# Sums of the MLP's weights: made once by GpSimd during attention and kept in DRAM, instead of made by GpSimd in every pass of the MLP

## The chip, the cores and the metric

The kernel runs on one core of a Trainium2 chip. The metric is the device time of one execution in microseconds. Everything is in float32. In the text PE is TensorE, DVE VectorE, ACT ScalarE, POOL GpSimd, and SP the queue from which nearly all DMAs are issued. L833 means line 833 of the kernel before.

## The reference, cut to what matters

An image of 48 x 48 tokens with 768 channels goes through a transformer block and then through a Fourier layer. The block is the part that the change touches:

```python
xn = layernorm(x, ln1_g, ln1_b)
q, k, v = split(xn @ qkv_w + qkv_b)                  # 12 heads of 64
attn = softmax(q * scale @ k.T + rel_h + rel_w)      # 2304 x 2304 per head
x = x + (attn @ v) @ proj_w + proj_b
xn2 = layernorm(x, ln2_g, ln2_b)
h = gelu(xn2 @ mlp_w1 + mlp_b1)                      # 2304 x 3072
x = x + (h @ mlp_w2 + mlp_b2)                        # 2304 x 768
# then: rfft2, two blockwise complex layers with relu and softshrink, irfft2, + x
```

## The kernel before

The program has five stages, one after the other, with the profile's times in microseconds: queries, keys and values (0 to 404), attention (404 to 1411), the projection (1411 to 1580), the MLP with the forward row transform (1580 to 2590), and the Fourier layer (to 2833).

**Seven products instead of eight.** The large matrix products cut both operands into 2 x 2 blocks and form the result from seven block products, not eight (the Strassen-Winograd scheme). For that, each operand needs sums and differences of its blocks. `left` (L160) makes those of a left operand with four additions, `right` (L166) those of a right operand: three new blocks, and one block that is overwritten. A weight chunk that is ready for use is thus seven blocks: four of the matrix (one of them overwritten) and three sums.

**Attention** is a loop over 6 pairs of heads (`pr`) and, within a pair, 6 groups of 384 queries (`c`), 36 iterations. An iteration has 18 steps `kt`. In each, PE makes the scores of 128 keys in `sp` (L670 content, L679 position, the latter from the tile `terms`), and ACT writes their exponentials to `exps`, which lies in `main` (L689). After every second step DVE adds two steps' exponentials into `pairs` (L833), and at the end the two halves of `pairs` into `acc` (L837). Then PE multiplies the exponentials with the values (L702) in six portions of three steps. Between the portions stands other work, by a table that `between` (L785) makes: before portion 1 DVE transposes `acc` and reduces it to `part` (`denominators`, L720 and L722); before portion 4 PE adds up the denominators with a small matmul that reads `part` (L731), DVE takes their reciprocal `rden` (L733), and POOL adds it to `inverse` (L735), which a later test for overflow reads; before portion 5 SP writes `rden` to DRAM (`den_d`, L749), stores an earlier result to `oT` (L783), and loads a broadcast of the reciprocals (`spread`, L762), after which DVE scales (L774) and POOL adds a bias (L777). The last of these stores is issued from POOL. For c below 3, and for c of 4 and 5 for the next pair, `relative` prepares the position terms of a coming iteration: matmuls into the one small PSUM bank, copies by ACT, a subtraction by DVE (L242), and 24 DMAs from SP for each `terms` (L309, L313), three buffers. The queries, keys and values of the next pair are loaded at c = 1 and c = 3.

**The order of work.** PE and SP keep the order of the program text throughout attention, and ACT and DVE in the loop, as the text asks for it (`manual_schedule`). POOL is not in that list during attention; a scheduler places its instructions. In the projection and in the MLP POOL is in the list.

**The projection** adds `proj_b` to the input on POOL (`residual`, L857) and then adds the products to that.

**The MLP** makes 3 passes of 768 tokens (`p`), each over 12 chunks of 256 hidden units (`n`). `weights(p, n)` (L1260) loads a chunk of `mlp_w1` (L1263) and one of `mlp_w2` (L1270), 768 KB each, and has POOL make the sums with `left` and `right`, eight additions of 128 x 384. Each chunk is loaded and summed anew in every pass. `hidden(p, n)` (L1280) makes seven products of three matmuls each (L1291), applies gelu (L1297) with the bias of two 128-unit tiles, `2 * n` and `2 * n + 1`, and has DVE make the sums of its result (`hs`). `added(p, n, i)` (L1333) multiplies with the chunk of `mlp_w2` (L1351, L1355) for three groups of tokens, and DVE adds to `x1` (L1353). It runs one chunk behind `hidden`, interleaved with it. The weight tiles have two buffers each, so that a chunk's loads are issued about a chunk ahead.

Of the kernel before, what the change touches and what calls it, by code (L numbers as in the profile page):

```python
# [19 lines left out]
P = 128  # L20
# [3 lines left out]
C = 768  # L24
# [3 lines left out]
FF = 4 * C  # L28
FCH = 256
TB = 768  # L30
G = 384
# [15 lines left out]
def block_then_afno(  # L47
# [6 lines left out]
    proj_w,  # L54
    mlp_w1,
    mlp_w2,
    vecs,
# [47 lines left out]
    stat_d = [dram.tile([12, P], F32, name=f"stat_d{p}") for p in range(T // TB)]  # L105
    den_d = dram.tile([NC * (T // G), 2 * G], F32, name="den_d")

    big1 = ctx.enter_context(tc.tile_pool(name="big1", bufs=1))
# [51 lines left out]
    def left(eng, a11, a12, a21, a22, s):  # L160
        eng.tensor_tensor(s[0], a21, a22, ALU.add)
        eng.tensor_tensor(s[1], s[0], a11, ALU.subtract)  # L162
        eng.tensor_tensor(s[2], a12, s[1], ALU.subtract)
        eng.tensor_tensor(a21, a11, a21, ALU.subtract)

    def right(eng, b11, b12, b21, b22, t):  # L166
# [28 lines left out]
    with ExitStack() as flag_scope:  # L195
# [12 lines left out]
        with ExitStack() as att:  # L208
# [444 lines left out]
            with tc.manual_schedule(engines={mybir.EngineType.PE, mybir.EngineType.SP}):  # L653
# [126 lines left out]
                def stored(queue=nc.sync):  # L780
                    while results:
                        pr, c, o = results.pop(0)
                        queue.dma_start(out=oT[ts(pr, P), ts(c, G)], in_=o)  # L783

                def between(pr, c, acc):  # L785

                    last = pr == NC - 1
                    work = {
                        1: [partial(denominators, pr, c, acc)],
                        4: [partial(inverses, pr, c)],  # L790
# [24 lines left out]
                with tc.manual_schedule(  # L815
                    engines={mybir.EngineType.Activation, mybir.EngineType.DVE}
                ):
                    for pr in range(NC):
                        for c in range(T // G):
# [8 lines left out]
                            pairs = o_pool.tile([P, 2, 2, G], F32, name="pairs", bufs=1)  # L828
                            for kt in range(NT):
                                scores(pr, c, kt, exps[:, kt])  # L830
                                if kt > 2 and kt % 2:
                                    so_far = exps[:, ds(0, 2)] if kt == 3 else pairs
                                    nc.vector.tensor_tensor(  # L833
                                        pairs, so_far, exps[:, ds(kt - 1, 2)], ALU.add
                                    )
                            acc = o_pool.tile([P, 2, G], F32, name="acc")
                            nc.vector.tensor_tensor(acc, pairs[:, 0], pairs[:, 1], ALU.add)  # L837
                            op = psum.tile([P, G], F32, name="op")
                            work = between(pr, c, acc)
                            for i in range(6):  # L840
                                for what in work.get(i, ()):
                                    what()
                                products(op, heads[pr][2], range(3 * i, 3 * i + 3))
                            finish(pr, c, op)
                    scaled(0)
                    stored(nc.gpsimd)
# [397 lines left out]
    with ExitStack() as mlp:  # L1244
# [15 lines left out]
        def weights(p, n):  # L1260

            w = wpool.tile([P, NC, FCH], F32, name="w1")
            nc.sync.dma_start(  # L1263
                out=w, in_=mlp_w1[:, ts(n, FCH)].rearrange("(c p) f -> p c f", p=P)
            )
            ws = wpool.tile([P, 3, 3, P], F32, name="w1s")
            a11, a12, a21, a22 = (w[:, ds(3 * j, 3), ts(i, P)] for i in range(2) for j in range(2))
            left(nc.gpsimd, a11, a12, a21, a22, [ws[:, i] for i in range(3)])
            v = wpool.tile([P, 2, C], F32, name="w2")
            nc.sync.dma_start(  # L1270
                out=v, in_=mlp_w2[ts(n, FCH), :].rearrange("(j p) c -> p j c", p=P)
            )
            vs = wpool.tile([P, 3, CH], F32, name="w2s")
            right(
                nc.gpsimd, v[:, 0, :CH], v[:, 0, CH:], v[:, 1, :CH], v[:, 1, CH:],
                [vs[:, i] for i in range(3)],
            )
            ready_w[p, n] = a11, a12, a21, a22, ws, v, vs

        def hidden(p, n):  # L1280

            a11, a12, a21, a22, ws, v, vs = ready_w.pop((p, n))
            h = hpool.tile([P, 2, TB], F32, name="hT")
            hs = hpool.tile([P, 3, G], F32, name="hs", bufs=1)
            kept[p, n] = h, hs, v, vs

# [9 lines left out]
            def gelu(i, k, src):  # L1296
                nc.scalar.activation(  # L1297
                    h[:, i, ts(k, G)], src, AF.Gelu, bias=col(V_B1 + 2 * n + i)
                )
# [6 lines left out]
            b11, b21, t3, b22, t1, t2, t4 = parts_of_tokens(xt, xs)  # L1306
            s1, s2, s4 = (ws[:, i] for i in range(3))
            product(0, a11, b11, True)
# [24 lines left out]
        def added(p, n, i):  # L1333

            h, hs, v, vs = kept[p, n]
            bank = [psum.tile([P, CH], F32, name=f"o{k}") for k in range(4)]
# [5 lines left out]
            s1, s2, s4 = (hs[:, k, ts(i, P)] for k in range(3))  # L1342
            b11, t3, b21, b22 = (v[:, f, ts(k, CH)] for f in range(2) for k in range(2))
            t1, t2, t4 = (vs[:, k] for k in range(3))
            t = 2 * (p * 3) + i
# [412 lines left out]
def _laid_out(x, given):  # L1758
# [24 lines left out]
    for i, name in enumerate(("L0_conv_rel_pos_h", "L0_conv_rel_pos_w")):  # L1783
        rel[:, i, : 2 * HW - 1] = w[name][::-1].T
    arrays = {
        "x": np.asarray(x).reshape(T, C),
# [4 lines left out]
        "proj_w": w["L0_conv_proj_w"],  # L1791
        "mlp_w1": w["L0_conv_mlp_w1"],
        "mlp_w2": w["L0_conv_mlp_w2"],
        "vecs": vecs,
# [34 lines left out]
```

## Time and profile before

| | us |
|---|---|
| median of 3 runs | 2832.62 |
| lowest and highest | 2831.85, 2834.68 |
| the profiled execution's own time | 2834.65 |
| its span, first to last instruction | 2832.9 |
| PE busy | 2788.5 |
| DVE busy | 1700.6 |
| ACT busy | 920.6 |
| POOL busy | 668.7 |
| DMA: bytes moved, mean rate | 269.09 MB, 95 GB/s |

A busy time is the time in which an engine ran instructions; issuing a DMA and waiting do not count. In a line of groups the order is: line, engine, operation, output and inputs by name, shapes, number of instructions, then the busy time, the mean of one in ns, and the idle time just before with what ended it. In a line of the timeline the order is: start, duration, engine, line, operation, operands, count, and in brackets the idle time before and what ended it. PEld is the loading of a matmul's stationary operand, which runs beside the matmuls. POOLq and SPq are the issue of DMAs on those queues.

### The profile page before, as it was taken

What the parts mean: (1) busy time and instruction counts of PE and PEld (TensorE: products, weight loads), DVE (VectorE), ACT (ScalarE), POOL (GpSimd) and SP (SyncE); (2) the same over time, 40 slices, a digit from 0 to 9 for tenths busy, and PEclk for the clock granted to TensorE, in tenths of its full rate; (3) what the DMA queues carried; (4) which work ended last, traced back from release to release, by engine and by line L of the source; (5) the groups of instructions that cost most, each with busy time, mean ns of one, the idle gap of its engine ahead of it and who ended that gap; (6) DMA issues with size and microseconds to landing.
All of it is one profiled execution on the core that took longest, in us unless ns stands there. A gap on an engine that the chain in (4) does not pass through costs nothing. (4 is left out here: it accounts for less than half of the span.)

```text
span 2832.9 us, 41042 instructions
## 1 busy us (share of the span) xinstructions
PE 2788.5 (98%) x15759; PEld 1716.2 (61%) x15759; DVE 1700.6 (60%) x2520; ACT 920.6 (32%) x1466; POOL 668.7 (24%) x662
## 2 busy tenths in 40 slices
PE   8999999999999999999999999999999999999998
PEld 4555655656656565665555555555555555556887
DVE  5434236767676767676756756565565566566665
ACT  1101135656566565665401201131101201102332
POOL 2505010000000000000164233342242422222432
PEclk9999999999999999999999999999999999999999
DMA  4535375273664737455332112131121212123254
GB/s 149 182 103 162 106 158 111 58 133 69 105 126 65 132 64 133 85 82 99 110 132 79 53 65 67 45 101 56 45 67 62 95 45 67 45 70 108 62 162 142
DMA packets 218430, 269.09 MB, mean 95 GB/s; under 512 B 24645, under 2 KB 197053, under 8 KB 216689
## 3 DMA queue, kind: packets, MB, share of 16 engines
q1 hardware_dynamic: 215720, 264.33, 37.5%
q8 instruction: 127, 2.08, 0.3%
q10 hardware_dynamic: 2440, 1.84, 0.2%
q14 instruction: 79, 0.64, 0.1%
q0 software_dynamic: 64, 0.20, 0.0%
HBM read 150.25 MB, written 52.32 MB: 72 GB/s over the span
## 5 line engine op out<-in xcount | busy, mean ns | idle before, releaser
L689 ACT ACTIVATE main<-sp 128x768 f32<-128x768 f32 x648 | 516.3, 812 | 34.5 <-PE sp L679 19.6
L833 DVE TENSOR_TENSOR pairs<-pairs,main 128x1536 f32<-128x1536 f32 x252 | 443.0, 1758 | 27.1 <-DVE pairs L833 0.9
L679 PE MATMUL sp<-terms,select 64*128 64x384 f32 x1296 | 412.0, 629 | 0.0
L1353 DVE TENSOR_TENSOR main<-o,main 128x384 f32<-128x384 f32 x540 | 298.7, 556 | 39.3 <-PE o L1351 1.2
L1291 PE MATMUL h<-shared,w 128*128 128x384 f32 x864 | 296.6, 486 | 0.7 <-POOL w2s L167 0.7
L670 PE MATMUL sp<-shared 64*128 64x384 f32 x1296 | 265.2, 485 | 1.6 <-ACT row_hi L241 1.0
L670 PE MATMUL sp<-qT,kT 64*128 64x384 f32 x1296 | 264.1, 484 | 0.0
L1291 PEld LDWEIGHTS h<-shared,w 128*128 128x128 f32 x864 | 163.9, 190 | 116.1 <-POOL w2s L167 1.3
L735 POOL TENSOR_TENSOR inverse<-inverse,rden 24x32 f32<-24x32 f32 x36 | 15.1, 421 | 926.5 <-DVE sums L734 887.5
L1291 PE MATMUL h<-shared,w1s 128*128 128x384 f32 x648 | 226.6, 486 | 0.0
L1297 ACT ACTIVATE hT<-c,vec 128x384 f32<-128x384 f32 x108 | 66.5, 615 | 465.1 <-DVE c L1303 465.0
L702 PE MATMUL op<-main,shared 128*64 128x384 f32 x1296 | 217.4, 488 | 0.0
L702 PE MATMUL op<-main,v 128*64 128x384 f32 x1296 | 216.4, 488 | 0.0
L833 DVE TENSOR_TENSOR pairs<-main 128x1536 f32<-128x1536 f32 x36 | 63.3, 1758 | 248.1 <-ACT main L689 248.1
L1303 DVE TENSOR_TENSOR c<-h,u 128x384 f32<-128x384 f32 x108 | 60.1, 557 | 212.4 <-PE h L1291 212.4
L1351 PE MATMUL o<-w,hT 128*128 128x384 f32 x432 | 174.8, 487 | 2.4 <-DVE mv L125 2.0
L1351 PE MATMUL o<-w2s,hs 128*128 128x384 f32 x432 | 174.9, 487 | 1.6 <-DVE hs L162 1.6
L679 PEld LDWEIGHTS sp<-terms,select 64*128 64x128 f32 x1296 | 125.3, 186 | 83.7
L1291 PEld LDWEIGHTS h<-shared,w1s 128*128 128x128 f32 x648 | 123.1, 190 | 85.8
L167 POOL TENSOR_TENSOR w2s<-w 128x384 f32<-128x384 f32 x36 | 35.9, 998 | 566.0 <-DMA w<-in_mlp_w_dram 424.0
L529 PE MATMUL m<-main 128*128 128x384 f32 x504 | 164.6, 488 | 2.4 <-DVE main L179 1.8
L702 PEld LDWEIGHTS op<-main,v 128*64 128x64 f32 x1296 | 96.9, 137 | 92.7 <-issue 67.7
(209 smaller groups left out, 4136.6 us busy)
## 6 DMA issues: line engine op xcount, KB each, us to landing
w<-in_mlp_w_dram SPq DMA_DIRECT2D x72, 768.0 KB
terms<-col_parts SPq DMA_DIRECT2D x432, 72.0 KB
terms<-row_hi SPq DMA_DIRECT2D x216, 72.0 KB
terms<-row_lo SPq DMA_DIRECT2D x216, 72.0 KB
main<-in_qkv_w_dram SPq DMA_DIRECT2D x36, 384.0 KB
z<-zt SPq DMA_DIRECT2D x48, 192.0 KB
x<-in_x_blocks_dram SPq DMA_DIRECT2D x18, 384.0 KB
k_d<-o SPq DMA_DIRECT2D x36, 192.0 KB
```

Of the source, the lines that this page charges most:

```text
L167: eng.tensor_tensor(t[0], b12, b11, ALU.subtract)
L529: nc.tensor.matmul(bank, a[:, c, :], b[:, c, :], start=(first and c == 0), stop=(c == 2), skip_group_check=not first,)
L670: nc.tensor.matmul(sp[:, j, :G], kT[at, ts(kt, P)], qT[at, ts(c, G)], start=first, stop=not first,)
L679: nc.tensor.matmul(sp[:, j, :G], select[at, a % 2], ready[pr, c][at, a // 2, b], start=first, stop=not first,)
L689: nc.scalar.activation(p, sp[:, :, :G], AF.Exp, scale=HD**-0.5)
L702: nc.tensor.matmul(op[ts(j, 64)], v[:, kt, ts(j, 64)], exps[:, kt, j, :], start=(kt == 0), stop=(kt == NT - 1),)
L833: nc.vector.tensor_tensor(pairs, so_far, exps[:, ds(kt - 1, 2)], ALU.add)
L1291: nc.tensor.matmul(bank[i], a[:, c, :], b[:, c, :], start=(start and c == 0), stop=(c == 2), skip_group_check=not start,)
L1297: nc.scalar.activation(h[:, i, ts(k, G)], src, AF.Gelu, bias=col(V_B1 + 2 * n + i))
L1303: nc.vector.tensor_tensor(t, src, other, ALU.add)
L1351: nc.tensor.matmul(bank[k], a, b, start=start, stop=True, skip_group_check=not start)
L1353: nc.vector.tensor_tensor(dst, bank[k], dst, ALU.add)
```

## The change

The two weight matrices are handed to the kernel in another order: `w1_blocks` and `w2_blocks`, arranged on the host as [chunk, third, 128 partitions, four blocks, 128]. Their values are the same. A chunk now takes its two 128-unit tiles from places four tiles apart (`tiles_of_chunk`), and the gelu's bias follows.

During attention 72 jobs run on POOL, two in each iteration: one for each of 12 chunks x 2 matrices x 3 thirds. A job has two parts. `asked` issues, on POOL's own queue, the load of four blocks into the tile `seven`, 256 KB. `summed` has POOL make the sums with `left` or `right`, four additions of 128 x 128, and issues on POOL's queue the write of all seven blocks to DRAM, 448 KB, as rows of 512 bytes (`w1_d`, `w2_d`). In an iteration the parts stand before step 2 (`asked`), before step 12 (`summed`), before portion 1 (`asked`) and after the last portion (`summed`). `seven` has one buffer, and so has `acc` now, which had two. POOL joins the engines that keep the order of the text in the attention loop.

In the MLP, `weights` loads the seven blocks of a chunk ready made, 1344 KB for each matrix; POOL's additions there are gone. The order of the instructions on PE, DVE and ACT, and the number and place of the loads on SP, are as before.

```diff
+    w1_d = [dram.tile([P, 7, 3, P], F32, name=f"w1_d{n}") for n in range(FF // FCH)]
+    w2_d = [dram.tile([P, 7, FF // (FCH * NS), CH], F32, name=f"w2_d{s}") for s in range(NS)]
...
+    def tiles_of_chunk(n):
+        half = FF // (2 * NS * P)
+        s, j = divmod(n, half)
+        return 2 * half * s + j, 2 * half * s + j + half
...
+                sum_jobs = [(k, n, i) for n in range(FF // FCH) for k in range(2) for i in range(3)]
+                in_hand = []
+
+                def asked():
+
+                    if not sum_jobs:
+                        return
+                    k, n, i = sum_jobs.pop(0)
+                    seven = o_pool.tile([P, 7, P], F32, name="seven", bufs=1)
+                    nc.gpsimd.dma_start(out=seven[:, :4], in_=(w1_blocks, w2_blocks)[k][n, i])
+                    in_hand.append((k, n, i, seven))
+
+                def summed():
+
+                    if not in_hand:
+                        return
+                    k, n, i, seven = in_hand.pop(0)
+                    (left, right)[k](
+                        nc.gpsimd, *(seven[:, a] for a in range(4)), [seven[:, a] for a in (4, 5, 6)]
+                    )
+                    s, j = divmod(n, FF // (FCH * NS))
+                    to = w2_d[s][:, :, j, ts(i, P)] if k else w1_d[n][:, :, i]
+                    nc.gpsimd.dma_start(out=to, in_=seven)
+
                 def between(pr, c, acc):
...
-                        1: [partial(denominators, pr, c, acc)],
+                        1: [asked, partial(denominators, pr, c, acc)],
...
-                    engines={mybir.EngineType.Activation, mybir.EngineType.DVE}
+                    engines={
+                        mybir.EngineType.Activation, mybir.EngineType.DVE, mybir.EngineType.Pool
+                    }
...
                             for kt in range(NT):
+                                if kt == 2:
+                                    asked()
+                                elif kt == 12:
+                                    summed()
                                 scores(pr, c, kt, exps[:, kt])
...
-                            acc = o_pool.tile([P, 2, G], F32, name="acc")
+                            acc = o_pool.tile([P, 2, G], F32, name="acc", bufs=1)
...
                             finish(pr, c, op)
+                            summed()
...
-            w = wpool.tile([P, NC, FCH], F32, name="w1")
-            nc.sync.dma_start(
-                out=w, in_=mlp_w1[:, ts(n, FCH)].rearrange("(c p) f -> p c f", p=P)
-            )
-            ws = wpool.tile([P, 3, 3, P], F32, name="w1s")
-            a11, a12, a21, a22 = (w[:, ds(3 * j, 3), ts(i, P)] for i in range(2) for j in range(2))
-            left(nc.gpsimd, a11, a12, a21, a22, [ws[:, i] for i in range(3)])
-            v = wpool.tile([P, 2, C], F32, name="w2")
-            nc.sync.dma_start(
-                out=v, in_=mlp_w2[ts(n, FCH), :].rearrange("(j p) c -> p j c", p=P)
-            )
-            vs = wpool.tile([P, 3, CH], F32, name="w2s")
-            right(
-                nc.gpsimd, v[:, 0, :CH], v[:, 0, CH:], v[:, 1, :CH], v[:, 1, CH:],
-                [vs[:, i] for i in range(3)],
-            )
-            ready_w[p, n] = a11, a12, a21, a22, ws, v, vs
+            w = wpool.tile([P, 7, 3, P], F32, name="w1")
+            nc.sync.dma_start(out=w, in_=w1_d[n])
+            v = wpool.tile([P, 7, CH], F32, name="w2")
+            g, j = divmod(n, FF // (FCH * NS))
+            nc.sync.dma_start(out=v, in_=w2_d[g][:, :, j])
+            ready_w[p, n] = w, v
...
-                    h[:, i, ts(k, G)], src, AF.Gelu, bias=col(V_B1 + 2 * n + i)
+                    h[:, i, ts(k, G)], src, AF.Gelu, bias=col(V_B1 + tiles_of_chunk(n)[i])
```

More of the change, by code (lines that the diff above doesn't have):

```diff
@@ L29 @@
 FCH = 256
+NS = 3
 TB = 768
@@ L54, in block_then_afno @@
     proj_w,
-    mlp_w1,
-    mlp_w2,
+    w1_blocks,
+    w2_blocks,
     vecs,
@@ L1260, in weights @@
         def weights(p, n):
-            w = wpool.tile([P, NC, FCH], F32, name="w1")
-            nc.sync.dma_start(
-                out=w, in_=mlp_w1[:, ts(n, FCH)].rearrange("(c p) f -> p c f", p=P)
-            )
-            ws = wpool.tile([P, 3, 3, P], F32, name="w1s")
-            a11, a12, a21, a22 = (w[:, ds(3 * j, 3), ts(i, P)] for i in range(2) for j in range(2))
-            left(nc.gpsimd, a11, a12, a21, a22, [ws[:, i] for i in range(3)])
-            v = wpool.tile([P, 2, C], F32, name="w2")
-            nc.sync.dma_start(
-                out=v, in_=mlp_w2[ts(n, FCH), :].rearrange("(j p) c -> p j c", p=P)
-            )
-            vs = wpool.tile([P, 3, CH], F32, name="w2s")
-            right(
-                nc.gpsimd, v[:, 0, :CH], v[:, 0, CH:], v[:, 1, :CH], v[:, 1, CH:],
-                [vs[:, i] for i in range(3)],
-            )
-            ready_w[p, n] = a11, a12, a21, a22, ws, v, vs
+            w = wpool.tile([P, 7, 3, P], F32, name="w1")
[4 more added lines that the diff above has]
+            ready_w[p, n] = w, v
         def hidden(p, n):
-            a11, a12, a21, a22, ws, v, vs = ready_w.pop((p, n))
+            w, v = ready_w.pop((p, n))
+            a11, a12, a21, a22, s1, s2, s4 = (w[:, i] for i in range(7))
             h = hpool.tile([P, 2, TB], F32, name="hT")
             hs = hpool.tile([P, 3, G], F32, name="hs", bufs=1)
-            kept[p, n] = h, hs, v, vs
+            kept[p, n] = h, hs, v
             bank = [psum.tile([P, G], F32, name=f"h{i}") for i in range(4)]
@@ L1306, in hidden @@
             b11, b21, t3, b22, t1, t2, t4 = parts_of_tokens(xt, xs)
-            s1, s2, s4 = (ws[:, i] for i in range(3))
             product(0, a11, b11, True)
@@ L1333, in added @@
         def added(p, n, i):
-            h, hs, v, vs = kept[p, n]
+            h, hs, v = kept[p, n]
             bank = [psum.tile([P, CH], F32, name=f"o{k}") for k in range(4)]
@@ L1342, in added @@
             s1, s2, s4 = (hs[:, k, ts(i, P)] for k in range(3))
-            b11, t3, b21, b22 = (v[:, f, ts(k, CH)] for f in range(2) for k in range(2))
-            t1, t2, t4 = (vs[:, k] for k in range(3))
+            b11, t3, b21, b22, t1, t2, t4 = (v[:, k] for k in range(7))
             t = 2 * (p * 3) + i
@@ L1784, in _laid_out @@
         rel[:, i, : 2 * HW - 1] = w[name][::-1].T
+    n_s, n_j = NS, FF // (FCH * NS)
     arrays = {
@@ L1791, in _laid_out @@
         "proj_w": w["L0_conv_proj_w"],
-        "mlp_w1": w["L0_conv_mlp_w1"],
-        "mlp_w2": w["L0_conv_mlp_w2"],
+        "w1_blocks": w["L0_conv_mlp_w1"]
+        .reshape(2, 3, P, n_s, 2, n_j, P).transpose(3, 5, 1, 2, 4, 0, 6)
+        .reshape(n_s * n_j, 3, P, 4, P),
+        "w2_blocks": w["L0_conv_mlp_w2"]
+        .reshape(n_s, 2, n_j, P, 2, 3, P).transpose(0, 2, 5, 3, 1, 4, 6)
+        .reshape(n_s * n_j, 3, P, 4, P),
         "vecs": vecs,
```

## The prediction

> **What bounds the kernel now.** The page's first part and the busy time by stage come first. Columns of the second: window, length, then busy us and instructions of PE, PEld, DVE, ACT, POOL, then clock, DMA share, GB/s.
>
> ```profile
> PE 2788.5 (98%) x15759; PEld 1716.2 (61%) x15759; DVE 1700.6 (60%) x2520; ACT 920.6 (32%) x1466; POOL 668.7 (24%) x662
> ...
> 404.00:1411.00 1007.00, 1006.38 (x8538) 604.22 (x8536) 676.71 (x567) 621.10 (x840) 56.60 (x70) 1.00 0.52 97
> ...
> 1580.00:2576.00 996.00, 991.47 (x3188) 579.75 (x3189) 605.42 (x1102) 134.29 (x236) 309.07 (x296) 1.00 0.19 63
> ```
>
> TensorE idles 0.6 us in attention (404 to 1411) and 4.5 us in the whole MLP (1580 to 2576), at full clock. So the MLP, whose POOL sums go away, has almost nothing to give back; attention, which receives POOL work, has only loss to offer. What stands right behind PE in attention? The groups and, from the timeline, the end of one iteration:
>
> ```profile
> L833 DVE TENSOR_TENSOR pairs<-pairs,main 128x1536 f32<-128x1536 f32 x252 | 443.0, 1758 | 27.1 <-DVE pairs L833 0.9
> ```
>
> ```profile
> 932.16 0.96 DVE L837 TENSOR_TENSOR acc<-pairs 128x768 f32<-128x768 f32 x1
> 933.03 0.55 DVE L242 TENSOR_TENSOR row_lo<-shared,row_hi 128x384 fp32r<-128x384 f32 x1
> 933.50 0.97 DVE L720 STREAM_TRANSPOSE turned<-acc 128x768 f32<-128x768 f32 x1
> 934.51 0.95 DVE L722 TENSOR_REDUCE part<-turned 128x24 f32<-128x768 f32 x1
> ...
> 935.98 0.12 PEld L731 LDWEIGHTS small<-gather,part 128*48 128x48 f32 x1 [0.18 <-issue]
> ```
>
> DVE adds the exponentials in pairs back to back (252 adds with 27.1 us idle before them in all, 0.1 us each), then `acc`, the transpose and the reduction; PE's small matmul L731 needs that reduction and sits in the middle of PE's stream. Here the reduction ends at 935.46 and PE comes at 935.98: 0.52 us to spare. Over the 36 iterations the trace gives 0.1 to 0.5 us of such slack for c = 0, 1, 2, about 1.7, 2.5 and 1.3 for c = 3, 4, 5, and 0.14 in the last three, where PE already waits. Any delay of DVE beyond that stops PE.
>
> **Which delays POOL causes.** The timeline just after attention, where POOL has similar work:
>
> ```profile
> 1413.95 1.35 DVE L880 TENSOR_TENSOR pws<-col_parts 128x1152 f32<-128x1152 f32 x1
> 1414.45 2.51 POOL L857 TENSOR_TENSOR main<-main,pb 128x768 f32<-128x768 f32 x1
> ...
> 1415.34 2.84 DVE L880 TENSOR_TENSOR pws<-pws,col_parts 128x1152 f32<-128x1152 f32 x1
> ...
> 1424.56 0.76 POOL L783 DMA_DIRECT2D oT<-o  x1 [0.31 <-POOL o L777]
> ```
>
> The POOL add, 1.8 us elsewhere, takes 2.51 because a DVE add of two SBUF operands is running; the next DVE add, 1.35 alone, takes 2.84: it stands still until POOL ends at 1416.96 and finishes 1.22 us later. The two take turns, one whole instruction each. The pair adds also have two SBUF operands.
>
> **The change, part by part.**
>
> *Removed in the MLP:* 288 POOL adds of about 1.0 us (36 chunks x 8). PE waits for them 0.7 us in all (the wait of L1291 on `w2s`). They also stretch some DVE adds at the MLP's start (`hs` 1.34 us against 0.56), where PE idles 3.8 us between 1550 and 1600. Gain: 3 us, bounds 0 and 8.
>
> *MLP loads* keep their number and place on SP's queue (72) but grow from 768 to 1344 KB. At 121 ns per 3072-byte packet on 16 engines one takes 3.4 us; two per chunk of 27.1 us, issued a chunk before use. About 20 us of cover: nothing. DMA share of that stage goes from 0.19 to at most 0.33.
>
> *Added in attention:* 72 jobs, two in each of 36 iterations, each a POOL load of 256 KB, four adds of 128x128, a POOL write of 448 KB in rows of 512 bytes. One buffer (`seven`) serves them all, so a job's load waits until the previous write has landed: each job is one serial chain. POOL is also held to program order now, so behind a waiting load stand `inverse` (L735) and the bias add of `o` (L777). Behind those: SP's store of `oT` (L783) and all that SP issues after it (the spread loads, the next `terms`); DVE's reciprocal (two `rden` buffers) and scaling (two `o` buffers). With about one to two iterations in hand a single delay hurts nobody, but POOL may not be slower than the loop: 1007 / 36 = 28.0 us.
>
> *One POOL add:* rows of 128x384 (1020 ns) and 128x1152 (2617 ns) give 2.08 ns per element, so 1020 - 256 x 2.08 = 0.49 us for 128.
>
> *Cost A, on DVE.* POOL runs one job's adds just after `inverse`, when DVE is idle; the other's fall about 8 to 14 us later, amid the next pair adds. Each of those four holds DVE 0.49 - 0.13 = 0.36 us (0.13 is the start-up that the 1.22 above shows hidden), 1.44 in sum. Less the slack: 18 x 0.92 (c below 3) + 5 x 0.12 (c = 5) + 3 x 1.30 (the last three) = 21 us of PE. None if all adds miss the pair adds; 66 us if both jobs meet them (2.9 us of delay: 42.5 + 6 + 2 + 8 + 8).
>
> *Cost B, POOL's own cycle.* The only POOL transfer in the trace is the last line above: landed 6.1 us after issue for 192 KB, its first packet 4.3 us after issue, with the DMA engines full (1.03). SP's small `den_d` writes show what load does: first packet 1.96 us after issue there, 1.15 in attention, 0.78 where engines are idle. I scale 4.3 x 1.15 / 1.96 = 2.5 us.
> Load: 2.5 + 1.1 (16 KB per engine, sharing) + 0.4 = 4.0; bounds 2.9 and 6.1.
> Write: 896 row descriptors instead of 128. If all of the issue's 0.76 us went by descriptor, 768 more cost 4.6 us; if none, 0; I take the middle, 2.3, as an instruction's start is in the 0.76 too. 2.5 + 2.3 + 2.4 (56 rows per engine at 28 ns, sharing) + 0.4 = 7.6; bounds 4.5 and 11.
> Adds: 2.0 for the free job; 5.4 for the other (2.0, and 0.9 + 1.4 + 1.1 behind pair adds); bounds 4 and 12 for both.
> `inverse` and `o`: 0.47 + 1.24.
> Cycle: 2 x (4.0 + 7.6) + 7.4 + 1.7 = 32.3 us, 4.3 more than the loop; x 36 = 155 us. The lag is not forgiven at the end, since POOL's residual adds (L857), which the projection needs, stand behind the last job. Bounds: 22.5 us (fits) and 48 us (+720).
>
> Here a rule speaks against the row. The Trainium skill, DMA: Bandwidth & Descriptors, Anatomy of one DMA (SWDGE path), fits a POOL transfer as 2.0 us plus bytes at 436 GB/s and calls descriptor building small: 2.6 and 3.05 us, a cycle of 2 x 5.65 + 7.4 + 1.7 = 20.4 us, and Cost B would be nothing. For the traced transfer it gives 2.45 us where 6.1 were measured. I stay near the row; the limit is load plus write of 9.5 us. A second place: SBUF (State Buffer), Who interferes with whom, infers that a DVE tensor_tensor does not hold up descriptor building, as it takes the shared read side alone. No line here shows it. Were it wrong, four issues per cycle would wait about 0.9 us each for an add: +3.5 us, 126 us more.
>
> *Moved:* POOL's order at attention's end. Before, a residual add (1410.91) stood ahead of the last `inverse`; now the last job, the last `o` and its store come first, some 6 us of POOL. POOL idles 52 us before L928 in that stage, which hides part: 4 us, bounds 0 and 10.
>
> *DMA engines:* the jobs add about 64,512 rows x 28 ns and 9,216 x 2 KB at 83 ns, 0.16 ms over 16 engines: attention's share goes from 0.52 to about 0.69. `terms` is issued an iteration or more ahead and no PE wait on it is listed: nothing.
>
> **Sum** on the profiled execution (2834.65; span 2832.9): + 155 (in which PE's waits of A disappear, since PE then waits for POOL) + 4 - 3 = 2990.7. The median of the runs lies 2.0 lower: 2988.6, so 2988.
>
> **Rivals.**
> (1) *POOL fits, DVE is delayed:* load plus write below 9.5 us. For it: the rule above, and DMA that is idle in two of six iterations. Against: the 6.1 row. 2834.65 + 21 + 4 - 3 - 2 = 2855, from 2843 to 2895.
> (2) *Nothing to measure (within 0.2%, 5.7 us, about what this measurement tells from no change):* POOL fits and each job's adds fall into DVE's free stretch, from the reduction to the next first pair add, some 9 us, so that DVE is delayed less than 0.5 us per iteration, the point from which it decides. It needs load plus write near 5 us, or a job so late that its adds pass `acc`. Against: half the cycle is busy pair adds. 2834.65 - 3 - 2 = 2830, not slower.
> (3) *Faster:* as (2), and the start and the pass changes of the MLP lose their DVE delays wholly, 8 us: 2825. PE's 4.5 us of idle time in the MLP speak against it.
>
> **Chances.** POOL overruns 0.57 (own range 2890 to 3180), (1) 0.28, (2) 0.10, (3) 0.05. Slower 0.85, same 0.10, faster 0.05. The range leaves out (2), (3) and the highest cycles: 2845 to 3170.
>
> **What would show it.** Right: POOL's share in attention rises from 6%, PE gets idle time in attention and its waits name DVE's `part`, POOL's `inverse` or SP's late `terms`; the loop lengthens to about 32 us after some iterations; POOL writes land over 7 us after issue; DVE's pair adds average above 1.76. Rival (1): loops of 28.5 us, waits on `part` alone. The MLP keeps 27.1 us a chunk in every case; if its windows shrink, or PE stays without a gap in attention, I am wrong. Wrong most likely in the descriptor build of the write and in the first-packet time, of which I have one row.

## The result, and the profile after

The changed kernel takes 2860.27 us (median of 4 runs, 2856.51 to 2876.46) against 2832.23 us before (4 runs, 2831.26 to 2834.68): the ratio is 1.0109, with a 95% interval from 1.0069 to 1.0148. It is slower, as forecast, but by 28 us and not by 156. The forecast was wrong in size. The profiled execution took 2856.51 us, the fastest of the four and 21.9 us over the profiled one of before; the stages below account for these 21.9 us, but for 0.4 us ahead of the first matmul.

In what follows lines are those of the changed kernel: a job's load is L802, its sums are L164 to L167 (`left`) or L175 to L178 (`right`), its write is L815; `inverse` is L743, the bias add of `o` L785, the store of `oT` L791, the pair adds L871, the small matmul of the denominators L739, the residual adds of the projection L896. In the experiments' kernels they shift by a few lines.

The page of the changed kernel first: busy time, the pair adds, and the two kinds of transfer (the last number is the median us from issue to landing).

```profile
PE 2795.7 (98%) x15759; PEld 1719.4 (60%) x15759; DVE 1719.9 (60%) x2520; ACT 920.0 (32%) x1466; POOL 804.8 (28%) x806
...
L871 DVE TENSOR_TENSOR pairs<-pairs,main 128x1536 f32<-128x1536 f32 x252 | 456.9, 1813 | 27.1 <-DVE pairs L871 0.9
...
w_d<-seven POOLq DMA_DIRECT2D x72, 448.0 KB, 4.6
...
seven<-in_w_blocks_dram POOLq DMA_DIRECT2D x72, 256.0 KB, 4.4
```

The pair adds are only 3% longer (1813 ns against 1758), and the waits further down show how little of that reaches PE. Where did the time go? Stage by stage, measured between the same matmuls in both traces (first scores; end of the last product with the values; first product of the MLP; end of the first pass). In the trace before, the first product of the MLP stands at 1554.36; the stage times given ahead, which end the projection at 1580, count the MLP's first 26 us to it.

| us | before | after | difference |
|---|---|---|---|
| attention | 1012.14 | 1017.35 | +5.2 |
| seam and projection | 139.16 | 161.39 | +22.2 |
| first pass of the MLP | 336.84 | 332.54 | -4.3 |
| rest of the MLP | 698.8 | 698.39 | -0.4 |
| queries, keys, values, and the Fourier layer | 637.82 | 636.61 | -1.2 |

The busy times by stretch (window, length, then busy us and instructions of PE, PEld, DVE, ACT, POOL, clock, DMA share, GB/s) show the same: attention is full, the projection is not, and its granted clock is 0.95.

```profile
404.00:1430.00 1026.00, 1017.23 (x8566) 608.46 (x8563) 696.52 (x567) 620.68 (x841) 468.57 (x489) 1.00 0.69 145
1430.00:1600.00 170.00, 151.61 (x472) 88.61 (x471) 105.31 (x185) 21.41 (x39) 82.04 (x64) 0.95 0.35 125
1600.00:2597.00 997.00, 991.58 (x3193) 580.13 (x3192) 608.38 (x1107) 134.62 (x238) 45.35 (x28) 1.00 0.28 102
```

The waits of the changed kernel (us in total, times, longest):

```profile
POOL seven L802 <- DMA w_d<-seven: 301.2, 71, 8.4
DVE total L1006 <- POOL inverse L743: 28.3, 1, 28.3
...
POOL inverse L743 <- DVE sums L742: 23.0, 6, 7.3
...
PE m L933 <- DMA og<-oT: 4.7, 1, 4.7
PE m L957 <- DVE ogs L176: 4.3, 1, 4.3
...
PE m L957 <- DVE main L937: 3.7, 1, 3.7
PE line L1028 <- DVE both L1010: 3.7, 1, 3.7
...
PE small L739 <- DVE part L730: 2.9, 2, 2.4
```

POOL waits 301 us for the landing of its own writes, 4.2 us per job. PE waits only 2.9 us for `part` in all of attention, but four times at the seam, 16.4 us in all: for `og`, a load of stored results, and for DVE's `both`, its add L937 and its `ogs`, which stand behind the wait for `inverse` on DVE. And DVE waits 28.3 us, a whole iteration, for POOL's last `inverse`. The timeline shows the end of attention, whose last product on PE ended at 1418.95:

```profile
954.75 1.97 POOL L167 TENSOR_TENSOR seven<-seven 128x128 f32<-128x128 f32 x1
...
1416.28 0.56 POOL L802 DMA_DIRECT2D seven<-in_w_blocks_dram  x1 [3.07 <-DMA w_d<-seven]
1416.84 0.27 POOL L743 TENSOR_TENSOR inverse<-inverse,rden 24x32 f32<-24x32 f32 x1
1417.08 1.25 POOL L785 TENSOR_SCALAR o<-o,vec 128x384 f32<-128x384 f32 x1
1418.36 0.33 SPq L791 DMA_DIRECT2D oT<-o  x1
1418.78 0.39 SPq L902 DMA_DIRECT2D og<-oT  x1
1419.16 0.45 POOL L175 TENSOR_TENSOR seven<-seven 128x128 f32<-128x128 f32 x1 [0.83 <-DMA seven<-in_w_blocks_dram]
...
1421.49 0.95 POOL L815 DMA_DIRECT2D w_d<-seven  x1 [0.40 <-POOL seven L178]
1423.68 18.25 PE L933 MATMUL m<-col_parts,og 128*128 128x384 f32 x48 [4.73 <-DMA og<-oT]
1430.83 0.55 POOL L802 DMA_DIRECT2D seven<-in_w_blocks_dram  x1 [8.39 <-DMA w_d<-seven]
...
1441.72 0.56 POOL L802 DMA_DIRECT2D seven<-in_w_blocks_dram  x1 [3.09 <-DMA w_d<-seven]
1442.28 1.82 POOL L896 TENSOR_TENSOR main<-main,pb 128x768 f32<-128x768 f32 x1
1444.04 0.27 POOL L743 TENSOR_TENSOR inverse<-inverse,rden 24x32 f32<-24x32 f32 x1
1444.34 0.19 DVE L1006 TENSOR_REDUCE total<-inverse 128x1 f32<-128x32 f32 x1 [28.30 <-POOL inverse L743]
1445.55 0.33 SPq L791 DMA_DIRECT2D oT<-o  x1
1445.63 0.27 PE L1028 MATMUL line<-ident,both 128*1 128x128 f32 x1 [3.69 <-DVE both L1010]
```

The last two iterations' `inverse` stand at 1416.84 and 1444.04. POOL is an iteration late: when attention is over, one job is half done and two have not begun. Around the last `inverse` stand the residual adds, and behind it the bias add and the last store of `oT`. The projection's first 48 matmuls (L933) need none of these, but even they start late: their load `og` stands on SP's queue behind a store of `oT` that waited for POOL's bias add (1417.08). What comes after them waits for the last `inverse` by way of DVE. Before, `inverse` ran 0.1 us after the reciprocal that it adds, 1.0 us in the last iteration. In the changed kernel this lag is 0.1 us for the first seven iterations, up to 14 until the eighteenth, and 28.6 us in the last. It does not rise evenly. On the whole it rises where the DMA engines are crowded and falls where they are quiet, as two pairs of jobs show (columns as above, DMA share last but one):

```profile
616.60:649.20 32.60, 32.60 (x248) 18.45 (x246) 23.38 (x20) 17.92 (x24) 13.03 (x15) 1.00 0.91 210
677.80:700.90 23.10, 23.10 (x190) 14.22 (x188) 14.98 (x13) 18.31 (x25) 12.69 (x15) 1.00 0.26 81
```

In the first pair of jobs one of the writes took 8.9 us to land; in the second, both landed in 3.6 us and the loads in 2.8.

Between the issue of one load and that of the next, the trace gives 14.63 us on average: 4.60 from the load's issue to the sums, 4.44 for the sums, 0.44 to the write's issue, 5.17 from there to the next load's. Two jobs are 29.3 us, and an iteration is 1012.14 / 36 = 28.1. Some 20 us of all the jobs' time, 11 of them in the first six iterations, are no work of the chain: POOL was ahead of the loop, and the sums, though their load had landed, stood behind an `inverse` or a bias add that had to wait for DVE (above, the wait of 23.0 us, part of which fell into a load's flight). Without this waiting the chain is 28.7 us for two jobs.

My theory: POOL's chain of two jobs is longer than the loop, by 1.1 to 1.2 us in the spacing of the jobs. The lag grows by what is not caught up, costs nothing at first, and is paid at the seam to the projection; beyond about two iterations it would stop the loop itself. The rivals: POOL's program order alone makes the seam late; the crowded transfers do; the contention of POOL and DVE does.

### The profile page after: what moved, and what is told of

It reads as the page before. It is cut to its first block, busy times and chain, and to the rows that moved or that the text cites. A ratio compares the mean times of both kernels' runs of the same rounds, so it can differ in the third digit from the quotient of the medians.

```text
span 2854.7 us, 41104 instructions
## 1 busy us (share of the span) xinstructions
PE 2795.7 (98%) x15759; PEld 1719.4 (60%) x15759; DVE 1719.9 (60%) x2520; ACT 920.0 (32%) x1466; POOL 804.8 (28%) x806
## 5 line engine op out<-in xcount | busy, mean ns | idle before, releaser
L1320 PE MATMUL h<-shared,w 128*128 128x384 f32 x1512 | 504.1, 486 | 0.7 <-issue 0.7
L871 DVE TENSOR_TENSOR pairs<-pairs,main 128x1536 f32<-128x1536 f32 x252 | 456.9, 1813 | 27.1 <-DVE pairs L871 0.9
L1320 PEld LDWEIGHTS h<-shared,w 128*128 128x128 f32 x1512 | 287.0, 190 | 202.0 <-issue 2.5
L1395 POOL TENSOR_TENSOR main<-main,acc 128x384 f32<-128x384 f32 x9 | 11.4, 1263 | 924.5 <-DVE main L1380 665.3
L1378 PE MATMUL o<-w,hs 128*128 128x384 f32 x648 | 262.5, 487 | 1.5 <-DVE hs L165 1.0
L1378 PE MATMUL o<-w,hT 128*128 128x384 f32 x648 | 245.1, 487 | 3.0 <-DVE main L1380 3.0
L871 DVE TENSOR_TENSOR pairs<-main 128x1536 f32<-128x1536 f32 x36 | 64.0, 1778 | 221.5 <-ACT main L697 221.4
L1378 PEld LDWEIGHTS o<-w,hT 128*128 128x128 f32 x648 | 122.7, 190 | 90.2 <-DVE main L1380 6.3
L1378 PEld LDWEIGHTS o<-w,hs 128*128 128x128 f32 x648 | 122.5, 190 | 89.5 <-DVE main L1380 4.9
L710 PEld LDWEIGHTS op<-main,shared 128*64 128x64 f32 x1296 | 96.5, 137 | 89.3 <-issue 64.4
```

The costliest lines, as they stand in the source:

```text
L710: nc.tensor.matmul(op[ts(j, 64)], v[:, kt, ts(j, 64)], exps[:, kt, j, :], start=(kt == 0), stop=(kt == NT - 1),)
L871: nc.vector.tensor_tensor(pairs, so_far, exps[:, ds(kt - 1, 2)], ALU.add)
L1320: nc.tensor.matmul(bank[i], a[:, c, :], b[:, c, :], start=(start and c == 0), stop=(c == 2), skip_group_check=not start,)
L1378: nc.tensor.matmul(bank[k], a, b, start=start, stop=True, skip_group_check=not start)
```

## Experiments

### Order alone, and two buffers

```diff
-                    engines={mybir.EngineType.Activation, mybir.EngineType.DVE}
+                    engines={
+                        mybir.EngineType.Activation, mybir.EngineType.DVE, mybir.EngineType.Pool
+                    }
```

This is the kernel before with POOL held to program order. 

> The kernel before, with POOL held to program order in the attention loop and nothing else changed. Theory L (the seam is slow because POOL reaches the end of attention a whole iteration late): no lag without jobs, so 2832 within 4 us, the projection stage near 139 us. Rival O (the order alone, which puts the last inverse and the last store ahead of the first residual add, costs the seam): 2845 to 2855, projection 152 to 161 us.

Measured: 2832.3 us against 2832.21, ratio 0.9998 (0.999 to 1.0006). The seam is 138.21 us, the lag 0.1 us. The order alone costs nothing.

```diff
-                    seven = o_pool.tile([P, 7, P], F32, name="seven", bufs=1)
+                    seven = o_pool.tile([P, 7, P], F32, name="seven", bufs=2)
```

The changed kernel with a second buffer. 

> The changed kernel with two buffers for the tile seven, so that a job's load need not wait for the previous write. Theory L: a job's chain loses the wait for the write, some 5 us of 14.6, the lag of inverse behind rden stays under 5 us at the end instead of 28.6, the projection falls from 161 to about 142 us, and the time to about 2840. Rival O, or a rival in which the crowded DMA engines at the seam are at fault: the projection stays above 155 us and the time above 2855.

Measured: 2831.32 us, ratio 0.9995 (0.9986 to 1.0003). The whole loss is gone: attention 1014.37, seam 137.95, MLP's first pass 332.86. The timeline of this kernel shows what the buffer takes away; a load is issued at once after a write:

```profile
952.43 0.94 POOL L815 DMA_DIRECT2D w_d<-seven  x1 [0.41 <-POOL seven L167]
953.25 0.70 POOL L802 DMA_DIRECT2D seven<-in_w_blocks_dram  x1
```

From a write's issue to the next load's it is 0.79 us instead of 5.17; the lag is never above 5.1 us. The sums, their place and all bytes are the same as in the changed kernel, and the writes land even later (5.2 us); `acc` has its one buffer here too. So neither the bytes nor the contention of POOL and DVE is the loss by itself. They lengthen the chain; beside that, they cost together the 2.2 us by which attention is still longer than before.

### Each half alone

The jobs in attention, with the MLP as before (it loads the matrices and makes its own sums):

```diff
-            w = wpool.tile([P, 7, 3, P], F32, name="w1")
-            nc.sync.dma_start(out=w, in_=w1_d[n])
...
+            w = wpool.tile([P, NC, FCH], F32, name="w1")
...
+            left(nc.gpsimd, a11, a12, a21, a22, [ws[:, i] for i in range(3)])
```

> The jobs run in attention as in the changed kernel, but the MLP loads and sums its weights as the kernel before does. Theory L: attention 1017 and projection 161 us as in the changed kernel, the MLP as before (337 us to the first row transform instead of 332.5), so about 2864. If the larger loads of the MLP cost something that its freed POOL hides, it is faster than the changed kernel, below 2857.

Measured: 2879.12 us (2870.35 to 2881.87), ratio 1.016 (1.0146 to 1.0175), more than expected. Here a job took 14.86 us. The seam was 160.41 us and attention 1034.44 us, with one gap of PE of 17.4 us near its end. This was the first sign that a lag of two iterations stops the loop.

The MLP's loads alone, without the jobs:

```diff
-                sum_jobs = [(k, n, i) for n in range(FF // FCH) for k in range(2) for i in range(3)]
+                sum_jobs = []
...
-            nc.sync.dma_start(out=w, in_=w1_d[n])
+            nc.sync.dma_start(out=w, in_=stand_in(n).rearrange("(p a c f) -> p a c f", p=P, a=7, c=3))
```

> No jobs in attention and POOL's order left to the scheduler as before; the MLP loads seven blocks of 1344 KB per matrix and makes no sums. The blocks are read from an input in place of the sums, so the MLP computes with other numbers than the reference. Theory L: attention and projection as before, the MLP's first stretch 4.3 us shorter, 2827 to 2828. If that difference was chance, 2832.

Measured: 2829.64 us, ratio 0.9992 (0.9984 to 1.0001), the MLP's first pass 332.54 us. What the change gives in the MLP is 4.3 us in the traces and 2.6 by the medians, with an interval that just takes in no change.

### The length of the chain: shorter, longer, and only its rows

Without the sums:

```diff
+                seven = o_pool.tile([P, 7, P], F32, name="seven", bufs=1)
+                nc.vector.memset(seven, 0.0)
...
-                    seven = o_pool.tile([P, 7, P], F32, name="seven", bufs=1)
...
-                    (left, right)[k](
-                        nc.gpsimd, *(seven[:, a] for a in range(4)), [seven[:, a] for a in (4, 5, 6)]
-                    )
```

> The changed kernel with one buffer, its 72 loads and 72 writes, but without the sums in attention: the tile is set to zero once, the loads overwrite four of its blocks and the write takes all seven. The three sums are thus zeros and the MLP's result is not the reference's; the number, the size and the place of all transfers stay. Theory L (POOL's serial chain of load, sums and write is a little longer than half an iteration): without the sums the chain is 14.6 - 4.4 = 10.2 us, two of them 20.4, less than the loop's 28.0; no lag grows, the last write is issued within 5 us of the end of attention, the seam before the first product of the MLP is 138 to 141 us, and the time 2828 to 2832 us. Rival T (the transfers themselves at the end of attention, or their crowding with the projection's, cost the 22 us): the seam stays at 155 to 161 us and the time at 2850 to 2857 us.

Measured: 2829.4 us (2825.96 to 2830.95), ratio 0.9988 (0.998 to 0.9997). Attention 1012.13 us, seam 137.88, lag 0.2 us. All transfers are there, with one buffer, and the loss is not: the rival that crowded transfers cost it by themselves falls. The last write is issued before the end of attention here; in the two kernels of the last experiment it is issued 8.6 and 8.8 us after it, and the seam is 138 us there too.

Three of four sums twice:

```diff
+                    for _ in range(2):
+                        if k:
+                            eng.tensor_tensor(s0, b, a, ALU.subtract)
+                            eng.tensor_tensor(s1, d, s0, ALU.subtract)
+                            eng.tensor_tensor(s2, c, s1, ALU.subtract)
...
```

> The changed kernel with one buffer, in which each job makes three of its four sums twice; the result is the same. Theory L: three more sums at 0.45 us alone to 1.3 us among pair adds, 1.4 to 3.9 us per job, make two jobs 29.3 + 5.3 = 34.6 us (32 to 37). The lag passes two iterations about a third of the way through attention, from there on POOL sets the loop's length, and the 36 iterations take about 36 x 34.6 = 1246 us in place of 1012 less what is still outstanding at the end: 2990 to 3080 us, and TensorE's waits name the reciprocal's late reuse. Rival P (POOL and DVE hinder each other, so that each sum costs DVE about 0.1 us): 216 more sums cost 15 to 30 us in attention, 2875 to 2890 us.

Measured: 2972.87 us (2968.5 to 2973.53), ratio 1.0493 (1.0477 to 1.051). A job took 16.24 us, less than I had expected, and the time lies below the expected range; the rival's 2875 to 2890 is far off. The waits of this kernel:

```profile
POOL seven L802 <- DMA w_d<-seven: 310.9, 71, 9.0
...
DVE rden L741 <- POOL inverse L743: 80.5, 23, 6.3
PE small L739 <- DVE part L730: 76.3, 11, 24.9
```

Now the loop hangs on POOL. The lag reaches 58 us in the seventh iteration and stays at 58 to 69 until the last four, the reciprocal waits for `inverse` 23 times, and PE waits 76.3 us for `part`.

The same bytes in longer rows:

```diff
-    w1_d = [dram.tile([P, 7, 3, P], F32, name=f"w1_d{n}") for n in range(FF // FCH)]
-    w2_d = [dram.tile([P, 7, FF // (FCH * NS), CH], F32, name=f"w2_d{s}") for s in range(NS)]
+    w1_d = [dram.tile([P, 3, 7, P], F32, name=f"w1_d{n}") for n in range(FF // FCH)]
+    w2_d = [dram.tile([P, 3, 7, P], F32, name=f"w2_d{n}") for n in range(FF // FCH)]
...
-                    to = w2_d[s][:, :, j, ts(i, P)] if k else w1_d[n][:, :, i]
-                    nc.gpsimd.dma_start(out=to, in_=seven)
+                    nc.gpsimd.dma_start(out=(w1_d, w2_d)[k][n][:, i], in_=seven)
```

> The changed kernel with one buffer, and the sums kept in DRAM as [128, 3, 7, 128], so that a job writes 128 rows of 3584 bytes in place of 896 rows of 512 bytes. The bytes are the same. If the number of rows sets the write's time (what the prediction gave 2.3 us for the building of descriptors, and the packets of 512 bytes at 28 ns), the issue falls from 0.93 to about 0.56 us and the landing from 4.6 to 3.5 to 4.0 us; two jobs are then 29.3 - 2 x 0.9 = 27.5 us, about the loop's 28.0, the lag stays below 15 us, the seam at 138 to 145 us and the time at 2830 to 2840 us. If only the fixed part of a transfer and the bytes set it, the job stays at 14.5 us, the lag at 25 to 30 us and the time at 2853 to 2858 us.

Measured: 2831.92 us (2827.38 to 2835.81), ratio 0.9998 (0.999 to 1.0007), with one buffer and all sums. The line of the writes on this kernel's page:

```profile
w_d<-seven POOLq DMA_DIRECT2D x72, 448.0 KB, 4.2
```

And from its timeline a write and the next load:

```profile
1360.76 0.56 POOL L813 DMA_DIRECT2D w_d<-seven  x1 [0.57 <-POOL seven L167]
1365.09 0.54 POOL L802 DMA_DIRECT2D seven<-in_w_blocks_dram  x1 [3.77 <-DMA w_d<-seven]
```

On average the write's issue fell from 0.93 to 0.58 us, and the time from there to the next load from 5.17 to 4.65. A job is 14.25 us instead of 14.63, less of a change than expected, and yet this is enough: the lag never exceeds 11.7 us, and attention and seam are 1.1 us longer than before.

### Which late product, and the kernel again

The add to `inverse` made by DVE:

```diff
-                    nc.gpsimd.tensor_tensor(inverse[:ND], inverse[:ND], rden, ALU.add)
+                    nc.vector.tensor_tensor(inverse[:ND], inverse[:ND], rden, ALU.add)
```

> The changed kernel with one buffer, and the small add to `inverse` of each iteration made by DVE in place of POOL. POOL keeps its jobs, the bias add and its store of `oT`. Theory L, first form (at the seam it is the reduction of `inverse` that is waited for): the seam falls from 161 us to 140 to 145 and the time to 2836 to 2842 us. Second form (it is the late store of `oT` and the residual adds behind the last job as well): the seam stays at 150 to 158 us, 2845 to 2855 us. In both the lag of POOL stays, with its last write 30 us after the end of attention.

Measured: 2871.08 us (2863.81 to 2875.7), ratio 1.013 (1.0114 to 1.0146). The time missed both expectations; the seam came as the second form of the theory had it. The job took 14.92 us here, and the waits show the loop stopped as well as the seam:

```profile
PE small L739 <- DVE part L730: 22.3, 2, 17.5
...
DVE o L782 <- POOL seven L176: 14.8, 1, 14.8
DVE main L937 <- POOL main L896: 8.8, 2, 7.1
...
PE m L933 <- DMA og<-oT: 3.7, 1, 3.7
```

The wait of `total` for `inverse` is gone, and the seam is still 157.36 us. The store of `oT` and the residual adds L896 are late as well. The seam has no single guilty product: each thing that POOL owes is an iteration late.

The changed kernel once more. 

> The changed kernel itself once more. Theory L: its time hangs on the mean job and moves from run to run, since one per cent of 14.6 us is 5 us per iteration pair over 36 iterations' 72 jobs, 10 us in all: runs from 2850 to 2880 us, median 2855 to 2862; the spread of the kernel before is 5 us. In the profile, the lag at the end of attention is 15 to 30 us with a seam of 150 to 162 us, and where the lag has passed two iterations (56 us) TensorE has a gap of over 10 us at the small matmul of the denominators.

Measured: 2869.35 us (2863.47 to 2874.03), ratio 1.0128 (1.0113 to 1.0144): the median is above the range that I had given, the gap came as expected. In this profile a job took 14.76 us, attention 1030.59 us and the seam 157.32. The lag reached 51.2 us. The waits of SP's queue in this profile:

```profile
SPq L791 <- POOL o L785: 105.6, 10, 19.4
```

The waits of the engines in it:

```profile
DVE o L782 <- DMA spread<-den_d: 56.1, 12, 19.2
...
PE small L739 <- DVE part L730: 13.6, 3, 13.1
```

And its timeline ahead of the gap of PE, which begins at 1386.6:

```profile
1375.48 1.26 POOL L785 TENSOR_SCALAR o<-o,vec 128x384 f32<-128x384 f32 x1
...
1376.76 0.33 SPq L791 DMA_DIRECT2D oT<-o  x1
1377.18 3.09 SPq L770 DMA_DIRECT2D spread<-den_d  x4
...
1380.95 0.56 DVE L782 TENSOR_TENSOR o<-ot,spread 128x384 f32<-128x384 f32 x1 [19.23 <-DMA spread<-den_d]
1381.43 1.75 DVE L871 TENSOR_TENSOR pairs<-main 128x1536 f32<-128x1536 f32 x1
```

This is how a late POOL stops PE. SP holds the store of `oT` until POOL has added the bias; the loads of `spread` stand behind that store on SP's queue; DVE's scaling waits for `spread`, and the pair adds stand behind the scaling; so `part` comes 13.1 us late for PE. It would also explain why the same kernel ran from 2856 to 2876 us, of which two runs have a profile: in one the lag stayed below 30 us and was paid mostly at the seam, in the other it came near two iterations first. Why a job takes 14.6 us in one run and 14.8 or 14.9 in another is not settled; its writes landed in 4.6, and in 4.9 us.

### Jobs where DVE is free

```diff
-                    seven = o_pool.tile([P, 7, P], F32, name="seven", bufs=1)
+                    seven = o_pool.tile([P, 7, P], F32, name="seven", bufs=2)
...
-                        1: [asked, partial(denominators, pr, c, acc)],
+                        1: [partial(denominators, pr, c, acc)],
...
-                                if kt == 2:
+                                if kt in (2, 3):
                                     asked()
-                                elif kt == 12:
-                                    summed()
...
                             summed()
+                            summed()
```

> The changed kernel with two buffers for the jobs, both loads asked for at the steps 2 and 3 of an iteration, and both jobs' sums after the iteration's last portion, in the stretch in which DVE makes no pair adds; the result is the same. Theory L with what remains of the delay of DVE: no lag beyond 5 us, the sums at 1.9 to 2.5 us per job in place of 4.4, attention 1012.1 to 1013 us (with two buffers alone it was 1014.4), the seam 138 us and the MLP 332.6 us: 2828 to 2830 us, as with the MLP's part alone (2829.6). If the two jobs back to back make the bias add and the last store late, lag 5 to 10 us and 2831 to 2834 us.

Measured: 2829.63 us (2826.96 to 2832.02) against 2832.99, ratio 0.9989 (0.9982 to 0.9996). Attention 1012.2 us, seam 138.14, MLP's first pass 332.54. The pair adds on its page:

```profile
L869 DVE TENSOR_TENSOR pairs<-pairs,main 128x1536 f32<-128x1536 f32 x252 | 447.1, 1774 | 27.1 <-DVE pairs L869 0.9
```

With the long rows as well: 

> As the kernel before it in this list, with the sums kept in DRAM as [128, 3, 7, 128], so that a job writes 128 rows of 3584 bytes; the result is the same. Two jobs then end some 1 us earlier; since nothing waits for them, 2828 to 2830 us, the same as without the long rows. If the write's rows disturb the loads of position terms or the matmuls, up to 1 us less.

Measured: 2831.46 us (2825.74 to 2833.81), ratio 0.9991 (0.9983 to 0.9999). The two are alike. The sums now cost POOL 3.1 us per job in the first of them and 2.7 in the second, not 4.4. Both keep the MLP's 4 us and lose nothing for it. Their intervals just leave out 1, but the gain is 0.1%.

## Why the prediction was wrong in size

**Mechanism right.** Cost B named it: one buffer makes each job a serial chain, POOL is held to its order, and POOL's lag is paid at the end of attention. The waits of e6 and e11 follow the path that it listed, `inverse` and the bias add, SP's store and the loads behind it, DVE's reciprocal and scaling. e2 and e5, which break the chain, lose nothing.

**The cycle, Cost B's first step, was 3.0 us too long.** For two jobs, in us:

| | predicted | measured |
|---|---|---|
| loads, issue to sums | 8.0 | 9.2 |
| writes, to the next load's issue | 15.2 | 11.2 |
| sums | 7.4 | 8.9 |
| `inverse` and bias add | 1.7 | 0 |
| cycle | 32.3 | 29.3 |

The cycle measured is the mean spacing and holds the 0.6 us in which POOL waited for the loop. The failed term is the write, 4.0 us too long for two; loads and sums, 1.2 and 1.5 us too short, hid part of it. I gave 2.3 us to the building of descriptors, as the middle between all and nothing of an issue's 0.76 us; in the changed kernel the write's issue is 0.93 us for 896 rows, the load's 0.56 us for 128, so 768 rows cost 0.4 us (e8 gives the same, 0.93 to 0.58 us for a write of the same bytes). `inverse` and the bias add are free, since they run while the second load is in flight (1416.84 and 1417.08 above, between the load's issue and its sums). The Trainium skill's rule (DMA: Bandwidth & Descriptors, Anatomy of one DMA, SWDGE path) was right that many descriptors cost little and too low in the sum: 2.6 and 3.05 us where the landing took 4.4 and 4.6. In the quiet pair of jobs above (DMA share 0.26) it was 2.8 and 3.6, so the larger part of the difference comes where the engines are crowded. Its cycle of 20.4 us would have meant no loss, my row's 32.3 gave 155; the chip's 29.3 lies nearer to the row.

**The multiplication, Cost B's second step, left out what is forgiven.** Seven kernels with one or two buffers can be set against (cycle - 28.1) x 36; the loss is that of attention and seam together, against 1151.3 us before:

| kernel | job | cycle | overrun x 36 | measured loss | forgiven |
|---|---|---|---|---|---|
| two buffers | 14.10 | 28.2 | 4 | 1.0 | |
| long rows | 14.25 | 28.5 | 14 | 1.1 | 13 |
| changed | 14.63 | 29.3 | 42 | 27.4 | 14 |
| changed, again | 14.76 | 29.5 | 51 | 36.6 | 15 |
| jobs alone | 14.86 | 29.7 | 58 | 43.6 | 15 |
| `inverse` on DVE | 14.92 | 29.8 | 63 | 46.4 | 16 |
| sums twice | 16.24 | 32.5 | 158 | 143.4 | 14 |

(The overrun is worked out from the unrounded job times. Kernels in which POOL keeps up and waits for the loop, 13.95 to 13.98 us a job, are left out; in the first two rows too it waits for the loop part of the time.) The job is the mean spacing of the loads in the same trace, so the overrun says how late POOL's last job was. The table is thus an account of one delay and no test of a rule; it shows that the end of the seam moves with the last job, less some 14 us. My step said that nothing is forgiven. Part of the 14 us is the last write's flight, 5.2 us that nobody waits for. The rest fits a slack that the trace before had at this place:

```profile
1412.68 0.56 POOL L735 TENSOR_TENSOR inverse<-inverse,rden 24x32 f32<-24x32 f32 x1
...
1415.78 15.75 PE L894 MATMUL m<-col_parts,og 128*128 128x384 f32 x48 [0.59 <-ACT ot L743]
1431.37 0.27 PE L989 MATMUL line<-ident,both 128*1 128x128 f32 x1
```

The last `inverse` was done at 1413.24, and the first product that needs it (L989, by way of `both`) came 18.1 us later, behind 48 matmuls that do not need it. In the changed kernel the same product (L1028) came 1.3 us after the end of `inverse`. Up to 17 us of lateness could thus be used up there; the exact sum with the other products that POOL owes is not shown.

The test of the multiplication is the kernel with its sums twice, in which POOL is behind from the second iteration on. It has almost the cycle that I had predicted, 32.5 for 32.3, and loses 143 us where I had 155. So of the 134 us by which the profiled time was overestimated (2990.7 against 2856.5), 109 are the cycle (3.04 x 36), 14 the forgiveness, 4 the loop's 28.0 for 28.1, 4 the step "Moved", which the measured loss already holds, and the rest small.

**Cost A was too large, as was its rival (1).** It gave each sum amid the pair adds 0.36 us of DVE. In the two-buffer kernel, pair adds that meet a sum take 1820 ns and the others 1758; 183 of the former for 152 sums make 0.07 us each. Attention lost 2.2 us there, not 21. Rival (1)'s 2855 comes near the measured time by luck, since its cause is another: PE waits 2.9 us for `part`, and POOL did not fit. The time lies in the stated range too, but in the part that stood for this rival; the range of the overrun alone began at 2890.

**Moved** (4 us): the order alone cost nothing (e1).

**MLP:** gain 4.3 us where 3 was taken and 8 was the bound; no load was waited for, with a DMA share of 0.28 where at most 0.33 was expected.

**What was to show it.** POOL's share in attention (46%), the longer pair adds and PE's waits on late products were right in kind. That the writes land over 7 us after issue was wrong (4.6), and so was the loop of about 32 us: attention is 5.2 us longer, 28.3 us an iteration, and most of the loss stands at the seam, which was not foreseen.

**Slips in the working.** The cycle's lower bound is 20.5 us by its own terms (2 x (2.9 + 4.5) + 4 + 1.7), not 22.5. The 83 ns of a 2 KB row stand in no line; they are an estimate between the traced rows of 512 and 3072 bytes (27 and 121 ns). And the DMA engines were idle in one of six iterations, not in two (share 0.05 from 684 to 712, but 0.40 from 656 to 684). None of this moves the forecast.

## What to carry to other kernels

When work is moved to an engine that "has time", set its serial chain per iteration, with every transfer's flight in it, against the loop: here a spacing of 29.3 against 28.1 us cost 27 us, 28.5 cost 1, and a second buffer took the chain apart. The mean is not all: two jobs took 23 us where the DMA engines were quiet and up to 36 where they were crowded, and time that the engine waits while it is ahead is not saved up for later. Near that balance a per cent of the job is worth 10 us and no forecast to a per cent is to be had, so give the range by the chain and look for the cheap edit that leaves it. A backlog is paid where the next stage first needs what the late engine owes, or earlier, where it outgrows the buffers.

## What the runs showed of the hardware

- A POOL sum of 128 x 128 takes 0.45 us alone and 1.63 us on average amid pair adds (the 1.97 us at 954.75 is one of them). POOL waits out up to a whole pair add, and then DVE loses only 0.07 us to it. I had read the turns as equal from a POOL add of 128 x 768 that held DVE for 1.49 us; for a short one almost all is hidden.
- POOL's issue of a write takes 0.93 us on average in the changed kernel, both amid pair adds (31 writes) and where DVE stands idle (20 writes). That DVE's two-operand adds do not hold up descriptor building, as the Trainium skill infers (SBUF — State Buffer, Who interferes with whom), agrees with this.
- At the seam the granted clock was 0.93 (1418.95 to 1580.34), against 0.98 before (1415.20 to 1554.36). PE idled 23.1 us there, against 7.4, and next to its gaps of 3.7 us and more the clock fell to about half for 3 to 7 us: 0.51 from 1422 to 1429, 0.52 from 1446 to 1453, 0.51 from 1456 to 1463 and 0.50 from 1504 to 1507. Before, there was one such gap, of 4.0 us, and 0.54 from 1475 to 1482. The first 48 matmuls took 18.25 us against 15.75. Of the seam's 22.2 us, 15.7 are longer gaps and 6.5 slower matmuls.
